# A planned order for a four-layer block on one core: idle products on TensorE in the first part, and another list of turns

## The chip, the core and the metric

The kernel runs on one NeuronCore of a Trainium2 chip. The metric is the device time of one execution in microseconds (us). The core has five engines that run their own instruction streams and meet at semaphores: TensorE (PE, whose weight loads are listed as PEld), VectorE (DVE), ScalarE (ACT), GpSimd (POOL) and SyncE (SP, which here only issues DMAs). [...]

## The reference

The input x has 16 sequences of 512 tokens by 256 features, all in f32. Each sequence passes four residual layers, each behind a layer norm, and no sequence needs another.

```python
x = x + attention(layernorm(x))     # 16 heads of 16, causal softmax, inner RMS norm
x = x + routed(layernorm(x))        # base product + shared low rank + 6 routed low ranks, best 2
x = x + scan(layernorm(x))          # conv of 4, silu, softplus; 16 states for each feature
x = x + routed(layernorm(x))        # the same weights as before

def scan_step(h, dt, bt, ct, xt):   # over 512 tokens
    h = exp(A * dt) * h + dt * xt * bt
    return h, sum_over_states(h * ct)
```

## The kernel before, in words

A sequence lies in SBUF as x with 4 tiles of 128 tokens. Its work is cut into some 376 steps (`plan.op`), each on one engine, each a small group of instructions with an estimated cost, the buffers that it reads and writes, and a place in PSUM or SBUF that it must hold. The functions `attention`, `routed` and `scan` only record the steps of one sequence; `order()` then plays all 16 sequences through at the estimated costs and puts out one order of all 6016 steps. A step is taken when its inputs are done, its engine is free and its buffers have places; among those that could go, the one with the smallest turn goes first. The turn is the sequence's entry of `STARTS` plus the step's entry of `TURNS`, which is one list of 376 numbers for all sequences. `OVER` and `CHANGE` are two more numbers of this rule (how far a kept engine may be overrun, and what a change of ScalarE's table counts). In the end the steps are issued in that order. The order is fixed at build time: on the chip each engine goes through its own list and waits where a semaphore is not yet there.

Up to four sequences are under way at a time, since x has four places. The places that matter here:

- PSUM has four banks called "one", for nearly everything (projections, transposes, sums, and the decays of the scan), and one group of four banks called "sc", for the attention scores of four heads.
- bc, the broadcast B and C of the scan, has one place. dd, what the scan works on, has five.

The steps around the change, with their lines:

- Attention makes the scores twice. First `four` (L566 the products of four heads into sc, L568 the mask added) is followed by a row maximum on VectorE (L637, into negm). The maxima are turned (L645) and added to the queries (qm, L650), the scores are made again (L566, L568), ScalarE takes the exponentials (L585, into pt), and L590 weighs the values with them. L601 turns the result back, L608 divides.
- `products` (L474) is the helper for all other products, so L474 stands for many of them: wq, wk, wv, wo, the base product and so on.
- `normalised` (L481 to L494): statistics on VectorE, a power on POOL, xh on ScalarE; L505 transposes xh, L508 copies it out of PSUM.
- The scan: SP writes dt and dt times x to DRAM (L816, L819), the small few too (L829), reads it back broadcast as bc (L830), and reads 32 slices dd of 512 KB broadcast over the states (L849). POOL multiplies (L856), ScalarE makes the decays into a bank "one" (L861), VectorE scans (L864), POOL multiplies again (L867), TensorE sums over states (L874), VectorE applies the gate (L880).
- Four groups of setup instructions (`setups`) are not steps of the plan. They are issued when the first step that needs them comes up. The second, `for_attention`, holds the loads and the scaling of the weights, and two products (L359, and wo with sg).

Of the kernel before, what the change touches and what calls it, by code (L numbers as in the profile page):

```python
# [10 lines left out]
F32 = mybir.dt.float32  # L11
# [6 lines left out]
P = 128  # L18
NEG = -1.0e30


OVER, CHANGE = 2.3, 97.0
STARTS = (
    0, 149, 234, 338, 413, 521, 619, 700, 790, 888, 996, 1074, 1174, 1263, 1369, 1447,
)
TURNS = (
    322, 924, 785, 870, 705, 84, 602, 525, 716, 736, 780, 829, 935, 688, 816, 888, 551, 888, 569, 780, 1037,
    1058, 780, 1053, 1052, 703, 823, 720, 796, 729, 794, 743, 758, 752, 822, 761, 826, 825, 945, 858, 844,
    656, 460, 479, 710, 820, 765, 711, 797, 755, 722, 823, 826, 738, 806, 840, 1808, 856, 863, 744, 849,
    851, 744, 788, 833, 754, 788, 766, 751, 859, 885, 1705, 883, 866, 807, 1037, 1066, 872, 1095, 1116, 757,  # L30
    814, 758, 845, 775, 829, 775, 854, 787, 878, 778, 819, 785, 833, 801, 850, 564, 392, 477, 669, 771, 810,
    720, 849, 837, 723, 824, 834, 729, 799, 814, 1625, 859, 798, 753, 898, 878, 758, 869, 924, 763, 873,
    814, 774, 828, 887, 1728, 845, 870, 913, 1017, 867, 1025, 795, 747, 619, 606, 834, 836, 824, 854, 204,
    875, 859, 701, 653, 760, 785, 601, 885, 649, 900, 844, 1052, 761, 625, 294, 465, 645, 644, 492, 604,
    701, 765, 811, 782, 660, 0, 531, 800, 645, 687, 566, 570, 613, 641, 518, 510, 470, 703, 660, 743, 1034,
    946, 605, 616, 676, 882, 619, 1044, 680, 1060, 712, 805, 957, 1000, 1101, 663, 941, 1101, 623, 890,
    1153, 849, 783, 616, 695, 622, 701, 684, 886, 650, 959, 803, 1136, 745, 727, 871, 1195, 973, 1019, 873,
    1211, 928, 818, 818, 937, 1046, 783, 1096, 904, 1208, 761, 767, 840, 962, 673, 1117, 931, 1159, 919,
    869, 880, 1059, 1081, 860, 1141, 944, 1257, 903, 867, 907, 1191, 989, 1264, 959, 1209, 1026, 890, 917,
    932, 1162, 952, 1293, 1071, 1366, 917, 930, 1018, 1268, 989, 1331, 1144, 1482, 1193, 1207, 930, 961,  # L40
    1168, 1480, 1042, 1195, 1009, 1344, 962, 968, 1052, 1231, 1060, 1264, 1093, 1321, 1019, 995, 969, 1128,
    1304, 1126, 1316, 1047, 1366, 973, 998, 1084, 1144, 1062, 1295, 1240, 1372, 1060, 993, 1019, 1122, 1311,
    1039, 1297, 1013, 1390, 1064, 1037, 1188, 1297, 1133, 1352, 996, 1349, 1058, 988, 1069, 1158, 1353,
    1153, 1350, 1021, 1424, 1076, 1045, 1055, 1230, 997, 1317, 1028, 1427, 999, 1130, 1032, 1059, 1037,
    1031, 1050, 1016, 1108, 1187, 528, 1091, 1082, 1153, 1067, 1132, 1266, 1209, 1446, 1077, 1275, 1141,
    1558, 1308, 1166, 904, 1004, 1071, 1242, 1188, 1479, 1564, 1511,
)


class Buf:  # L50


    def __init__(self, plan, res, make):
        self.plan, self.res, self.make = plan, res, make
        self.tile, self.users, self.taken = None, 0, False
        self.done = {}
# [11 lines left out]
class Plan:  # L68
# [5 lines left out]

    def __init__(self, places):
        self.places, self.ops, self.seq, self.stage = dict(places), [], 0, 0
# [46 lines left out]
    def order(self):  # L126

        first = {}
        for o in self.ops:
            o.turn = STARTS[o.seq] + (TURNS or [0] * len(self.ops))[o.num - first.setdefault(o.seq, o.num)]  # L130
        free, busy, table, link, port = dict(self.places), {}, None, 0.0, False
        kept = {}
        ready = {}
        for o in self.ops:
            ready.setdefault(o.eng, [])
            busy.setdefault(o.eng, False)
            if not o.left:
                bisect.insort(ready[o.eng], (o.turn, o.num, o))
        events, out = [], []
        now, tick = 0.0, 0  # L140
        while True:
            for eng, heap in ready.items():
                if busy[eng] or not heap:
                    continue
                until, what = kept.get(eng, (None, None))

                picked, turns = None, heap
                if eng == "ACT":
                    turns = sorted(heap, key=lambda i: (i[0] + CHANGE * (i[2].table not in (None, table)), i[1]))
                for item in turns:  # L150
                    if until is not None and not self.wanted(item[2], what):
                        cost = item[2].cost + 1.3 * (item[2].table not in (None, table))
                        if now + cost > until + OVER:
                            continue
                    need = {}
                    for b in item[2].bufs:
                        if not b.taken:
                            need[b.res] = need.get(b.res, 0) + 1
                    if not (item[2].port and port) and all(free[k] >= v for k, v in need.items()):
                        picked = item[2]  # L160
                        heap.remove(item)
                        break
                if picked is None:
                    continue
                o = picked
                for b in o.bufs:
                    if not b.taken:
                        b.taken = True
                        free[b.res] -= 1
                cost = o.cost  # L170
                if o.table is not None:
                    cost += 1.3 * (o.table != table)
                    table = o.table
                if until is not None and self.wanted(o, what):
                    del kept[eng]
                if isinstance(o.then, Op):
                    kept[o.then.eng] = (now + cost + o.lat, o.then)
                elif o.then is not None:
                    kept[o.then[0]] = (now + cost + o.lat, o.then[1])
                busy[eng] = True  # L180
                port = port or o.port
                out.append(o)
                end = now + cost
                done = end + o.lat
                if o.load:
                    link = max(link, end) + o.load
                    done = link + o.lat
                tick += 2
                heapq.heappush(events, (end, tick, "free", o))
                heapq.heappush(events, (done, tick + 1, "done", o))  # L190

            late = [eng for eng, (at, what) in kept.items() if at + 0.3 < now and not busy[eng]]
            for eng in late:
                del kept[eng]
            if late:
                continue
            if not events:
                if not kept:
                    break
                kept.clear()  # L200
                continue
            now = events[0][0]
            while events and events[0][0] <= now:
                _, _, kind, o = heapq.heappop(events)
                if kind == "free":
                    busy[o.eng] = False
                    if o.port:
                        port = False
                    continue
                for b in o.bufs:  # L210
                    b.users -= 1
                    if not b.users:
                        free[b.res] += 1
                for x in o.after:
                    x.left -= 1
                    if not x.left:
                        bisect.insort(ready[x.eng], (x.turn, x.num, x))
        assert len(out) == len(self.ops), "operations wait for each other's places"
        self.span = now
        return out  # L220


@with_exitstack
def tile_block(ctx: ExitStack, tc: tile.TileContext, a: dict, out: bass.AP):
# [4 lines left out]
    nc = tc.nc  # L229
# [16 lines left out]
    ps = ctx.enter_context(tc.tile_pool(name="ps", bufs=1, space=PSUM))  # L246
# [5 lines left out]
    def tile_of(name, shape, dtype=F32):  # L252
        return const.tile(shape, dtype, name=name)
# [7 lines left out]
    ident, identb = tile_of("ident", [P, P]), tile_of("identb", [P, P], BF)  # L261
# [166 lines left out]
    banks = {"one": (4, [P, 512]), "sc": (1, [P, G, 512])}  # L428
# [3 lines left out]
    plan = Plan(places)  # L432
# [463 lines left out]
    with tc.manual_schedule():  # L896
        done = 0
        for o in plan.order():

            while done < o.stage:  # L900
                setups[done]()
                done += 1
            o.fn()


# [44 lines left out]
```

## Time and profile before

| | before |
|---|---|
| time, median of 3 runs | 2061.71 us (2060.84 to 2065.83) |
| the profiled execution, its own time | 2066.51 us |
| its span, first to last instruction | 2064.7 us |
| busy PE / DVE / POOL / ACT | 1801.9 / 1513.4 / 1371.1 / 1194.0 us |
| mean granted TensorE clock | 0.954 |
| DMA | 316.35 MB, 153 GB/s mean |

Busy times are sums over the span, for one profiled execution. The page's slices cut the span into 40 equal parts and give each engine's busy share in tenths, with the granted TensorE clock (PEclk) below. A timeline row gives start, duration, engine, line, operation, operands and count; brackets hold the idle time just before it and what ended it. In the trace an f32 product that is no transpose appears as two records.

### The profile page before, as it was taken

How to read it: one execution, taken by the hardware profiler on the slowest of the kernel's cores; microseconds unless marked ns; L12 is line 12 of the kernel's file. 1: busy time of each engine (PE TensorE's matmuls, PEld its weight loads, DVE VectorE, ACT ScalarE, POOL GpSimd, SP SyncE). 2: the span in 40 equal slices, each digit the busy share in tenths (PEclk: the TensorE clock that was granted, in tenths of full speed). 3: DMA queues.
4: the chain of work that ended last, by engine and by line, in shares of the span. 5: the costliest groups of instructions: out<-in, count | busy, mean ns of one | idle time of the engine just before them, and what ended most of it. 6: DMA issues, size and time to landing. Idle time of an engine off the chain costs nothing. (4 is left out here: it accounts for less than half of the span.)

```text
span 2064.7 us, 34733 instructions
## 1 busy us (share of the span) xinstructions
PE 1801.9 (87%) x13253; PEld 953.8 (46%) x13253; DVE 1513.4 (73%) x2479; ACT 1194.0 (58%) x1685; POOL 1371.1 (66%) x814
## 2 busy tenths in 40 slices
PE   4788789999999999999999999999999999996455
PEld 2244344555455454545455454545554454544123
DVE  4335677878788787878788787878788787876563
ACT  2236556565666757565666667575666766564431
POOL 3001784949587685859597785859596785848693
PEclk8789899999999999999999999999999999998766
DMA  3000956848494866847494867849493957747791
GB/s 93 1 1 22 216 122 155 197 127 210 109 233 109 216 164 167 205 137 191 110 231 100 225 153 175 204 120 212 110 231 95 228 143 186 183 125 183 186 222 31
DMA packets 113064, 316.35 MB, mean 153 GB/s; under 512 B 17809, under 2 KB 36610, under 8 KB 112898
## 3 DMA queue, kind: packets, MB, share of 16 engines
q1 hardware_dynamic: 112194, 313.99, 62.5%
q8 instruction: 105, 1.72, 0.4%
q14 instruction: 61, 0.50, 0.1%
q10 hardware_dynamic: 704, 0.14, 0.0%
HBM read 287.87 MB, written 26.21 MB: 152 GB/s over the span
## 5 line engine op out<-in xcount | busy, mean ns | idle before, releaser
L864 DVE TENSOR_TENSOR_SCAN dd<-one,dd 128x512 f32<-128x512 f32 x512 | 607.9, 1212 | 185.2 <-ACT one L861 88.3
L856 POOL TENSOR_TENSOR dd<-dd,bc 128x1024 f32<-128x1024 f32 x256 | 603.6, 2361 | 194.0 <-DMA dd<-drows 156.8
L867 POOL TENSOR_TENSOR dd<-dd,bc 128x1024 f32<-128x1024 f32 x256 | 601.9, 2358 | 86.2 <-DVE dd L864 80.4
L637 DVE TENSOR_REDUCE negm<-sc 128x4 f32<-128x512 f32 (+3 forms) x256 | 380.4, 1486 | 154.0 <-PE sc L568 153.7
L861 ACT ACTIVATE one<-dd,am 128x512 f32<-128x512 f32 x512 | 344.3, 689 | 249.4 <-DVE dd L864 108.9
L585 ACT ACTIVATE pt<-sc 128x2048 f32<-128x2048 f32 (+3 forms) x256 | 316.3, 1235 | 189.0 <-PE sc L568 187.8
L487 POOL TENSOR_SCALAR rs<-mv 128x4 f32<-128x4 f32 x64 | 12.3, 193 | 364.2 <-DVE mv L482 361.4
L566 PE MATMUL sc<-qm,kT 32*128 32x512 f32 (+3 forms) x2048 | 214.1, 488 | 37.8 <-ACT pt L585 28.4
L566 PE MATMUL sc<-kT,qT 32*128 32x128 f32 (+3 forms) x2048 | 217.0, 494 | 30.5 <-DVE negm L637 25.9
L568 PEld LDWEIGHTS <-identb 128*128 128x128 bf16 x2048 | 117.4, 98 | 232.4 <-issue 217.2
L874 PE MATMUL one<-dd,ysel 128*32 128x512 f32 x1024 | 172.7, 633 | 55.5 <-POOL dd L867 46.4
L590 PE MATMUL one<-pt,vv 128*32 128x512 f32 (+3 forms) x2048 | 191.6, 449 | 8.1 <-DVE dd L864 7.9
L566 PEld LDWEIGHTS sc<-qm,kT 32*128 32x128 f32 x2048 | 80.9, 185 | 181.5 <-ACT pt L585 120.4
L474 PE MATMUL one<-base,xtR 128*128 128x256 f32 x512 | 139.5, 395 | 18.6 <-DVE dd L864 18.0
L566 PEld LDWEIGHTS sc<-kT,qT 32*128 32x128 f32 x2048 | 82.0, 187 | 156.8 <-DVE negm L637 63.3
L494 ACT ACTIVATE xhR<-x,nm,rs 128x256 f32<-128x256 f32 x192 | 99.4, 588 | 53.2 <-POOL nm L490 53.1
L528 DVE TENSOR_TENSOR x<-one,x 128x512 f32<-128x512 f32 x128 | 86.4, 675 | 34.7 <-PE one L474 34.5
L474 PEld LDWEIGHTS one<-base,xtR 128*128 128x128 f32 x512 | 94.5, 194 | 36.8 <-DVE dd L864 21.5
L481 DVE BATCH_NORM_STATS2 st<-x 128x6 f32<-128x256 f32 x256 | 103.7, 405 | 4.8 <-DMA x<-in_x_dram 4.1
L568 PE MATMUL sc<-mask_q,identb 128*128 128x128 bf16 x1024 | 103.7, 225 | 0.0
L568 PE MATMUL sc<-mask_k,identb 128*128 128x128 bf16 x1024 | 102.8, 224 | 0.0
L505 PE MATMUL one<-ident,xhR 128*128 128x128 f32 x384 | 61.9, 290 | 35.2 <-ACT xhR L494 27.7
(132 smaller groups left out, 2449.4 us busy)
## 6 DMA issues: line engine op xcount, KB each, us to landing
dd<-drows SPq DMA_DIRECT2D x512, 512.0 KB
x<-in_x_dram SPq DMA_DIRECT2D x16, 512.0 KB
drows<-dt SPq DMA_DIRECT2D x32, 256.0 KB
drows<-sg SPq DMA_DIRECT2D x32, 256.0 KB
bc<-brows SPq DMA_DIRECT2D x16, 512.0 KB
out_dram<-x SPq DMA_DIRECT2D x16, 512.0 KB
brows<-few SPq DMA_DIRECT2D x16, 64.0 KB
wo<-in_Wo_dram SPq DMA_DIRECT2D x2, 256.0 KB
```

Source lines behind the costliest of these rows:

```text
L474: nc.tensor.matmul(o[:, lo:hi], lhsT=lhsT, rhs=rhs, start=n == 0, stop=n == len(todo) - 1)
L481: nc.vector.bn_stats(st()[:, t, :], x()[:, t, :])
L566: nc.tensor.matmul(sc()[:, g, 0:n], lhsT=lhsT(g), rhs=rhs(g), start=True, stop=False)
L568: nc.tensor.matmul(sc()[:, g, at : at + P], lhsT=identb, rhs=mask, start=False, stop=True)
L585: o.then = op("ACT", act(G * n), lambda pt=pt, sc=sc, n=n: nc.scalar.activation(pt(), sc()[:, :, 0:n], AF.Exp), r=[sc], w=[pt], table="exp")
L590: nc.tensor.matmul(av()[rows(g), kt * P : T], lhsT=vals()[:, kt, G * j + g, :], rhs=pt()[:, g, :], start=kt == 0, stop=kt == NT - 1,)
L637: o.then = op("DVE", dve(G * n), lambda t=t, n=n, sc=sc, nm=nm, s=s: nc.vector.tensor_reduce(nm()[:, t, :, 1 - s, 0:1], sc()[:, :, 0:n], A ...
L856: op("POOL", pool(1024), lambda dd=dd: nc.gpsimd.tensor_tensor(dd()[:, :, 1, :], dd()[:, :, 1, :], both(0), ALU.mult), port=True, r=[(bc, ...
L861: op("ACT", act(512) + 0.07, lambda i=i, k=k, dd=dd, dec=dec: nc.scalar.activation(dec(), dd()[:, i, 0, :], AF.Exp, scale=am[:, k + 4 * i ...
L864: op("DVE", 1.22, lambda i=i, dd=dd, dec=dec: nc.vector.tensor_tensor_scan(dd()[:, i, 1, :], dec(), dd()[:, i, 1, :], 0.0, ALU.mult, ALU.a ...
L867: op("POOL", pool(1024), lambda dd=dd: nc.gpsimd.tensor_tensor(dd()[:, :, 1, :], dd()[:, :, 1, :], both(1), ALU.mult), port=True, r=[(bc, ...
L874: nc.tensor.matmul(sums()[rows(g), :], lhsT=ysel[:, m, :], rhs=four[g]()[:, g % 2, 1, :], start=m == 0, stop=m == 3)
```

## The change

The list of turns and the starts are replaced, with `OVER` and `CHANGE`. The other part is new: `order()` now also keeps the stretches in which TensorE is busy in the played schedule and how many banks "one" are free over time. `resting` goes through the schedule's first part (to `START`, in the schedule's own time) and looks at each rest of TensorE: where a rest is long enough for an idle product, a bank "one" is free, and TensorE was busy for less than a set share of the time just before, it counts one idle product for the step that follows. When the steps are issued, each such product multiplies the identity with itself, 256 columns in f32, into a bank "one" that nothing reads. This makes 63 idle products. None is issued ahead of the first setup.

```diff
-OVER, CHANGE = 2.3, 97.0
-STARTS = ( 0, 149, 234, 338, 413, 521, 619, ...
-TURNS = ( 322, 924, 785, 870, 705, 84, ...
+OVER, CHANGE = 2.2, 380.0
+STARTS = ( 0, 388, 628, 931, 1235, 1513, ...
+TURNS = ( 964, 2212, 2292, 2200, 2062, 1448, ...
...
+    SPAN, BUSY, IDLE, EDGE, START = 3.4, 0.72, 0.45, 0.1, 330.0
...
+        runs, room = [], [(0.0, free["one"])]
...
+                if eng == "PE":
+                    runs.append((now, end, o))
...
+        self.rests = self.resting(runs, room)
         return out
+
+    def resting(self, runs, room):
+        rests, last, at, k = {}, [], 0.0, 0
+        for begin, end, o in runs:
+            if begin > self.START:
+                break
+            while at + self.IDLE + self.EDGE <= begin:
+                while k + 1 < len(room) and room[k + 1][0] <= at:
+                    k += 1
+                i, free = k + 1, room[k][1]
+                while i < len(room) and room[i][0] < at + self.IDLE + self.EDGE:
+                    free = min(free, room[i][1])
+                    i += 1
+                last = [x for x in last if x[1] > at - self.SPAN]
+                worked = sum(b - max(a, at - self.SPAN) for a, b in last)
+                if free > 0 and worked < self.BUSY * self.SPAN:
+                    rests[o.num] = rests.get(o.num, 0) + 1
+                    last.append((at, at + self.IDLE))
+                    at += self.IDLE
+                else:
+                    at += self.EDGE
+            last.append((begin, end))
+            at = max(at, end)
+        return rests
...
                 setups[done]()
                 done += 1
+            for _ in range(plan.rests.get(o.num, 0) if done else 0):
+                one = ps.tile([P, 512], F32, tag="one", name="one", bufs=banks["one"][0])
+                nc.tensor.matmul(one[:, 0 : 2 * P], lhsT=ident, rhs=ident.unsqueeze(1).to_broadcast([P, 2, P]), start=True, stop=True)
             o.fn()
```

The new order is close to the old one. Sequences begin and end at nearly the same shares of TensorE's steps; of 1520 steps on TensorE 85% stand in the same order as before, on VectorE 68%, on ScalarE 74%, on POOL and SP 81 and 82%. In the changed kernel all lines from the class Plan on are some 5 to 43 lower down in the file; the texts use the numbers of the kernel before unless they say otherwise.

## The prediction

> **What bounds the kernel now.** I read the page's slices first, to split the run into stages; then the busy time and clock of each stretch of 50 us; then TensorE's own waits in the middle; then the timelines of the two ends. The page's slices:
>
> ```profile
> PE   4788789999999999999999999999999999996455
> PEclk8789899999999999999999999999999999998766
> ```
>
> There are three stages: a first part of some 330 us in which TensorE is neither full nor at full clock, a middle to about 1850 us at nine tenths and more, and a tail. Stretches of 50 us (busy PE, PEld, DVE, ACT, POOL, then clock, DMA share, GB/s):
>
> ```profile
> 50.00:100.00 50.00, 36.74 (x272) 15.17 (x276) 13.93 (x13) 14.32 (x15) 0.00 (x0) 0.74 0.00 1
> 100.00:150.00 50.00, 41.27 (x310) 20.72 (x303) 13.89 (x28) 17.25 (x21) 0.00 (x0) 0.82 0.00 1
> ...
> 1100.00:1150.00 50.00, 47.65 (x348) 25.56 (x347) 38.76 (x67) 33.64 (x50) 24.99 (x21) 1.00 0.41 108
> ...
> 1950.00:2000.00 50.00, 22.41 (x91) 11.20 (x89) 31.06 (x51) 16.89 (x28) 45.25 (x23) 0.71 0.95 221
> ```
>
> From 50 to 150 us TensorE is busiest by far and runs at 0.74 and 0.82 of its clock, while GpSimd and DMA do nothing. In the middle TensorE bounds at full clock. In the tail it is GpSimd (45 of 50 us). TensorE's timeline shows how the clock is lost:
>
> ```profile
> 96.17 1.24 PE L566 MATMUL sc<-kT,qT 32*128 32x256 f32 x8 [2.38 <-DVE negm L637]
> 97.34 0.60 PE L568 MATMUL sc<-mask_q,identb 128*128 128x128 bf16 x4
> 99.26 1.66 PE L566 MATMUL sc<-kT,qT 32*128 32x384 f32 x8 [1.32 <-DVE negm L637]
> ...
> 114.27 3.73 PE L474 MATMUL one<-xtA,wq 128*128 128x512 f32 x4
> 117.93 0.93 PE L566 MATMUL sc<-qm,kT 32*128 32x384 f32 x8
> ```
>
> The tile sc exists once, so product and row maximum alternate, and TensorE rests in every maximum. The granted clock is 0.50 from 94 to 118 us: the product of 384 columns takes 1.66 us at 99.26 and 0.93 at 117.93. All of this lies on the path. In the middle, TensorE's own waits from 350 to 1850 us (total, times, longest) are:
>
> ```profile
> PE sc L566 <- ACT pt L585: 20.8, 66, 2.0
> PE one L474 <- DVE dd L864: 18.0, 13, 1.4
> PE one L645 <- DVE dd L864: 9.2, 13, 0.9
> PE one L590 <- DVE dd L864: 7.0, 12, 0.6
> ```
>
> The last three wait for a PSUM bank "one" that a scan on VectorE still holds, once in each sequence. The loads of x that wait for a place run from 400.4 to 1670.6 us in 11 steps, so a sequence takes 115.5 us.
>
> **The change part by part.** 1. *Idle products.* The changed program has 63 of them, 256 columns in f32. Four such real products (wv, 33.03 us) take 1.95 us, so one costs 0.49 us warm; at half clock the two of wo,sg took 2.08 us with their latency, so about 0.97.
>
> What they can win is the cold work repriced at its own warm rows. 44.6 to 66.4 us: products, masks, turns and the wq projection sum to 15.99 us cold and 9.06 warm, 6.9 less. 96.2 to 117.9: the same mix, 6.9 less. 214 to 225: 3.3. 251 to 254: 1.6. 285 to 292: 2.8. In the first two nothing else is busy, so I count 13.8 in full. The other three (7.7) lie beside the first scans, where the DMA share is about 1.0 and POOL fills up; I count half, 3.9, and keep 0 and 7.7 as ends.
>
> [...] With one to three idle products in each maximum (the order has 3 behind a score product of 512 columns, 1 behind one of 128 or 256, 2 or 3 behind 384), these stretches rise from below 0.6 to about 0.75 busy. They fit: the gaps at warm rates are 0.8, 1.3, 1.9 and 2.4 us against 0.49 to 1.47.
>
> What they cost. *The start.* 19 of them stand behind wo,sg and ahead of the first transposes of xhA. The schedule's own times know nothing of the setup, and on the chip those transposes do not wait for data: xhA is ready at 10.8 us.
>
> ```profile
> 20.80 1.80 PE L505 MATMUL one<-ident,xhA 128*128 128x128 f32 x8
> ...
> 25.32 3.37 PE L474 MATMUL one<-xtA,wq 128*128 128x512 f32 x4
> 28.49 3.95 PE L474 MATMUL one<-xtA,wk 128*128 128x512 f32 x8
> 32.37 0.50 PE L566 MATMUL sc<-kT,qT 32*128 32x128 f32 x8
> ```
>
> From 21.0 us: the clock came back after 6 us of gapless work (111.85 to 117.9), so four are cold (3.9 us) and 15 warm (7.4): transposes at 32.3. Then four transposes 0.6, copy 0.59, three xhA activations that ScalarE now has between the two copies 1.55, copy 0.59, and wk, wq, four transposes, wk at warm rates 6.5: first score product at 42.2 instead of 32.4, 9.8 later less small overlaps, so +9.5. Behind the last idle product stand all of attention's products; VectorE and ScalarE wait for those. *The other 44.* Those in maxima are covered by VectorE's reduce; without that cover each is 0.49. 11 of them wait for a bank that ScalarE or VectorE must release, the last around the first scans. No row shows such a wait; the nearest is a real product's wait for L864, 0.5 to 2.2 us in the first part. I take +2 in all (0 to 8).
>
> Sum of the first part: -13.8 -3.9 +9.5 +2 = -6.2. The middle is bound by TensorE, so the shift reaches the end.
>
> 2. *The order in the middle.* Each engine keeps its instructions[...]. Three moves bear on the shown waits. The value product behind a score product is moved one score product later (L590), which puts 0.64 us of filler (pt of 256 columns) just ahead of the L474 base product that waits 1.4 for its bank. On VectorE the gate product L880, which frees the bank "sums", goes ahead of the two qm steps, so the 0.7 us waits at L645 may shrink. Against it, scans are now grouped two and two ahead of row maxima, so a maximum may come 1.2 us (one L864) later, with sc and all of TensorE behind it. SP's loads of dd follow the new order of POOL, at equal numbers. Ends: -2 us (all three bank waits gone, and some of pt) to +2 (a new wait of 1.2 to 2.4); I take -0.5 for 13 sequences, -6.5, near the filler's size.
>
> 3. *The tail.* The load of bc for the last sequence waits for its only buffer:
>
> ```profile
> 1937.82 4.63 POOL L867 TENSOR_TENSOR dd<-dd,bc 128x1024 f32<-128x1024 f32 x2 [2.94 <-DVE dd L864]
> 1947.17 2.35 POOL L856 TENSOR_TENSOR dd<-dd,bc 128x1024 f32<-128x1024 f32 x1 [4.72 <-DMA bc<-brows]
> 1952.97 2.34 POOL L856 TENSOR_TENSOR dd<-dd,bc 128x1024 f32<-128x1024 f32 x1 [3.45 <-DMA dd<-drows]
> ```
>
> SP issues it at 1942.47, when L867 ends. Two dd loads stand ahead of it now; in the changed order they stand behind it, with the second drows write (L819), and land two transfers later (0.5 MB at the 230 GB/s of the slices is 2.3 us each). POOL then starts at about 1951.8 and is fed 3 us later for good. POOL's order before that point is also changed and may end sequence 14 earlier; waits of 4.33, 1.83 and 2.94 us stand there. I take +1.5 (-6 to +5).
>
> Sum: -6.2 -6.5 +1.5 = -11.2. The profiled execution spans 2064.7 us and took 2066.5, 0.2% above the median of 2061.7; against the median this gives 2050.
>
> **The rivals.** *A better middle.* If the order takes 1.5 us off each sequence's 6 us of waits, 13 times: -19.5 -6.2 +1.5, 2038, and 2034 with the late cold stretches in full. For it: bank waits are what the moves touch. Against it: the moves are of one place mostly.
>
> *Slower: a new wait in the middle.* A pair of scans (2.4 us) ahead of a row maximum that TensorE waits for, in each of 13 sequences. At 1.5 us each it is +19.5 -6.2 +1.5: 2076. It decides from 1.0 us a sequence on, where it outweighs the first part beyond 0.3%. For it: a maximum's release of sc is already a wait of TensorE's weight loads. Against it: in the middle, TensorE itself waited for negm once.
>
> *Only the cost.* The clock stays low in spite of the idle products, or TensorE's saving runs into the scans: +9.5 +4, 2075. [...] *It cancels.* The changed program has the products, but the start's 9.5 eats the gain and the order is neutral: 2060.
>
> **How the numbers follow.** A measurement of this kernel tells 0.3%, 6.2 us, from no change. Forecast (2040 to 2058) 0.42, of it 0.05 within 0.3%; better middle 0.16; cancels 0.11; new wait 0.22; only the cost 0.09. Faster 0.53, same 0.16, slower 0.31. The range 2027 to 2077 leaves out a tenth on either side; the forecast's own range is 2040 to 2058.
>
> **What would show it.** Right: clock 1.00 from 35 to 330 us; the first score product at about 42 us, and the wq projection that ended at 118 us some 4 us earlier; a sequence at 115.0 us; the last scan's first POOL step waiting for dd, not bc. Wrong: transposes at 21 us (the 19 are hidden), clock 0.5 in the maxima, a period of 116 us or more, or new waits of idle products for banks near 300 us.

## The result, and the profile after

| | before | after |
|---|---|---|
| time, median of 4 runs each | 2061.97 us (2060.84 to 2065.83) | 2028.09 us (2024.89 to 2031.13) |
| ratio, 95% interval | 1 | 0.9832 (0.9812 to 0.9852) |
| span of the profiled execution | 2064.7 us | 2023.1 us |
| mean granted TensorE clock | 0.954 | 0.973 |

The change makes the kernel 33.9 us faster by the medians. The direction was forecast, the size (11.2 us) was not. The two profiled executions differ by 41.6 us, because the one before is 4.5 us slower than its median and the one after 3.2 us faster. So a shift read from the traces is up to some 8 us too large at the end. It can also be off at a single point: five later runs with the old order in the first 200 us (m2 to m6 below) have the last exponential of sequence 0 at 129.2 to 131.8 us, the profile before has it at 134.1. Ratios are used for sizes, traces for places.

Lines of the changed kernel are 40 higher from attention on (L864 is L904, L566 is L606 and so on); the idle products are L945. The page's slices of the changed kernel, TensorE's busy share and its clock:

```profile
PE   5889889999999999999999999999999999996544
PEclk9999999999999999999999999999999999998866
```

The clock is at nine tenths or more in the first 36 slices; before, four of the first five stood at 7 or 8. Stretches of 50 us of the changed kernel (PE, PEld, DVE, ACT, POOL, clock, DMA share, GB/s):

```profile
50.00:100.00 50.00, 40.37 (x345) 19.93 (x344) 18.69 (x17) 14.34 (x15) 0.00 (x0) 1.00 0.00 1
100.00:150.00 50.00, 42.95 (x352) 23.95 (x352) 17.94 (x34) 18.87 (x25) 2.65 (x5) 1.00 0.00 1
```

From 50 to 150 us the clock went from 0.74 and 0.82 to 1.00, and TensorE is busy 5 us longer, with idle products among its work. POOL already has its first work before 150 us. TensorE's timeline in the maxima, at the place shown before:

```profile
96.01 0.71 PE L606 MATMUL sc<-kT,qT 32*128 32x256 f32 x8 [1.03 <-DVE negm L677]
...
96.89 0.65 PE L945 MATMUL one<-ident 128*128 128x256 f32 x2
...
109.50 1.94 PE L514 MATMUL one<-xtA,wq 128*128 128x512 f32 x4
```

One idle product (two records) stands in the maximum, the wait behind it is short, and the products have their warm durations: 0.71 us where there were 1.24, and wq 1.94 where it took 3.73. The start of TensorE's timeline shows the price:

```profile
20.82 10.24 PE L945 MATMUL one<-ident 128*128 128x256 f32 x38
30.89 1.04 PE L545 MATMUL one<-ident,xhA 128*128 128x128 f32 x8
...
39.94 0.50 PE L606 MATMUL sc<-kT,qT 32*128 32x128 f32 x8
```

The 19 products ahead of the first transposes last 10.24 us, and the first score product begins at 39.94 us instead of 32.37. TensorE's own waits from 400 to 1800 us, first before, then after (us in total, times, longest):

```profile
PE one L474 <- DVE dd L864: 16.7, 12, 1.4
PE one L645 <- DVE dd L864: 8.3, 12, 0.9
PE one L505 <- DVE dd L864: 6.6, 13, 0.5
PE one L874 <- issue: 6.0, 12, 0.5
...
PE one L874 <- POOL dd L867: 2.2, 12, 0.2
```

```profile
PE one L514 <- DVE dd L904: 13.1, 24, 1.1
PE one L914 <- POOL dd L907: 12.0, 24, 1.1
PE one L545 <- DVE dd L904: 10.4, 24, 0.6
...
PE one L685 <- DVE dd L904: 6.8, 12, 0.9
```

The bank waits have not gone: the three for VectorE's scans come to 31.6 us before and 30.3 after. The longest of L474 fell from 1.4 to 1.1 us, that of L645 stayed at 0.9, the waits of xhR's transposes (L505, now L545) grew, and the waits of the sums over states (L874, now L914) went from 8.2 us (6.0 of them "issue", which the profile puts down to nothing) to 12.0 for POOL. Yet the loads of x that wait for a place now run from 394.5 to 1648.8 us in 11 steps, 114.0 us for a sequence instead of 115.5. Six more traces below with this order in the middle (e2, e3, e4, f1, f2, s2) give 114.1 to 114.3 us, four with the old one (e1, m3, m5, s1) 115.4 to 115.7; so the gain is nearer to 1.3 us a sequence. From the first exponential of sequence 3 to that of sequence 15, twelve sequences, before and after (us, busy PE, PEld, DVE, ACT, POOL, clock, DMA share, GB/s):

```profile
398.71:1784.73 1386.02, 1305.38 (x9937) 697.27 (x9938) 1123.42 (x1825) 889.29 (x1260) 1025.46 (x601) 1.00 0.70 170
```

```profile
382.30:1751.57 1369.27, 1296.05 (x9936) 696.24 (x9936) 1117.41 (x1825) 887.81 (x1261) 1025.21 (x601) 1.00 0.71 172
```

In these two traces TensorE is idle for 0.6 us less in each sequence, and busy for 0.8 us less with the same work. Most of the busy part is in the sums over states: L874 alone is busy for 118.4 us of this stretch before and 110.2 after.

Where the shift arises, by each sequence's first exponential (L585), the first and last POOL step of a scan, and the end; the runs e1 and e2 below split the change into its two parts:

| us | before | after | idle products alone | order alone |
|---|---|---|---|---|
| last pt of sequence 0 | 134.1 | -6.0 | -6.6 | -3.5 |
| scan of sequence 0, first step | 214.7 | -6.3 | -6.0 | -4.1 |
| scan of sequence 0, last step | 311.4 | -21.1 | -9.6 | -16.7 |
| first pt of sequence 3 | 398.7 | -16.4 | -10.1 | -12.4 |
| first pt of sequence 15 | 1784.7 | -33.2 | -8.2 | -27.1 |
| scan of sequence 14, last step | 1940.1 | -43.3 | -7.5 | -37.1 |
| scan of sequence 15, first step | 1947.2 | -35.2 | -7.5 | -28.4 |
| end | 2064.7 | -41.6 | -8.9 | -35.6 |

### The profile page after: what moved, and what is told of

Read it like the earlier page. It is cut to its first block, busy times and chain, and to the rows that moved or that the text cites. A ratio compares the mean times of both kernels' runs of the same rounds, so it can differ in the third digit from the quotient of the medians.

```text
span 2023.1 us, 34985 instructions
## 1 busy us (share of the span) xinstructions
PE 1794.7 (89%) x13379; PEld 962.0 (48%) x13379; DVE 1504.3 (74%) x2479; ACT 1189.4 (59%) x1683; POOL 1371.1 (68%) x814
## 5 line engine op out<-in xcount | busy, mean ns | idle before, releaser
L904 DVE TENSOR_TENSOR_SCAN dd<-one,dd 128x512 f32<-128x512 f32 x512 | 607.1, 1211 | 182.2 <-ACT one L901 84.3
L677 DVE TENSOR_REDUCE negm<-sc 128x4 f32<-128x1024 f32 (+3 forms) x256 | 380.0, 1484 | 166.1 <-PE sc L608 166.0
L606 PE MATMUL sc<-qm,kT 32*128 32x512 f32 (+3 forms) x2048 | 210.3, 480 | 27.1 <-ACT pt L625 20.7
L606 PE MATMUL sc<-kT,qT 32*128 32x128 f32 (+3 forms) x2048 | 210.3, 480 | 20.9 <-DVE negm L677 16.7
L914 PE MATMUL one<-dd,ysel 128*32 128x512 f32 x1024 | 167.3, 632 | 63.2 <-POOL dd L907 48.6
L608 PEld LDWEIGHTS <-identb 128*128 128x128 bf16 x2048 | 115.6, 97 | 224.8 <-issue 209.4
L630 PE MATMUL one<-pt,vv 128*32 128x512 f32 (+3 forms) x2048 | 186.5, 443 | 7.7 <-DVE dd L904 7.6
L606 PEld LDWEIGHTS sc<-qm,kT 32*128 32x128 f32 x2048 | 80.0, 182 | 161.2 <-ACT pt L625 114.8
L606 PEld LDWEIGHTS sc<-kT,qT 32*128 32x128 f32 x2048 | 80.0, 182 | 148.6 <-DVE negm L677 50.3
L514 PEld LDWEIGHTS one<-base,xtR 128*128 128x128 f32 x512 | 92.9, 191 | 34.2 <-DVE dd L904 20.9
L545 PE MATMUL one<-ident,xhR 128*128 128x128 f32 x384 | 61.6, 291 | 38.6 <-ACT xhR L534 26.5
```

The lines of the kernel that those rows point to most:

```text
L514: nc.tensor.matmul(o[:, lo:hi], lhsT=lhsT, rhs=rhs, start=n == 0, stop=n == len(todo) - 1)
L606: nc.tensor.matmul(sc()[:, g, 0:n], lhsT=lhsT(g), rhs=rhs(g), start=True, stop=False)
L608: nc.tensor.matmul(sc()[:, g, at : at + P], lhsT=identb, rhs=mask, start=False, stop=True)
L630: nc.tensor.matmul(av()[rows(g), kt * P : T], lhsT=vals()[:, kt, G * j + g, :], rhs=pt()[:, g, :], start=kt == 0, stop=kt == NT - 1,)
L677: o.then = op("DVE", dve(G * n), lambda t=t, n=n, sc=sc, nm=nm, s=s: nc.vector.tensor_reduce(nm()[:, t, :, 1 - s, 0:1], sc()[:, :, 0:n], A ...
L904: op("DVE", 1.22, lambda i=i, dd=dd, dec=dec: nc.vector.tensor_tensor_scan(dd()[:, i, 1, :], dec(), dd()[:, i, 1, :], 0.0, ALU.mult, ALU.a ...
```

## The experiments

**The two parts apart.** Edits: e1 keeps the changed program and gives it the old lists; e2 keeps the new lists and drops the idle products.

```diff
 e1_idle_only
-OVER, CHANGE = 2.2, 380.0      (STARTS and TURNS likewise)
+OVER, CHANGE = 2.3, 97.0
 e2_order_only
-        return rests
+        return {}
```

Expected of e1: 

> The order of the kernel before, with the idle products added by the same rule (again 63, nearly at the same places). Theory A (the forecast's own split: clock saving less the cost of the 19 at the start, and the rest of the gain is the order): about 6 us faster than before, 2056; TensorE's clock 1.00 in the first part, the first exponential of sequence 3 (362.5 us before, 346.8 after) at about 356, the middle at 115.5 us a sequence, and the tail as long as before. Theory B (the idle products are worth all of the 16 us gained in the first part, the late cold stretches in full): about 17 us faster, 2045, that exponential at about 347.

Expected of e2: 

> The changed order without any idle product. Theory A: 28 us faster than before, 2034; the clock falls to 0.5 in the first part as before, yet the filling of the pipeline from 240 to 350 us is about 10 us shorter than before, the middle takes 114.0 us a sequence, the tail is 8 us shorter. Theory B: 17 us faster, 2045: middle and tail as in the changed kernel, nothing gained before 350 us.

(The 362.5 and 346.8 us in the first of these are the last exponential of sequence 2. The first one of sequence 3 is at 398.7 us before, at 382.3 after and at 388.6 in e1.)

Measured: e1 0.9969 (0.9959 to 0.9979), 6 us faster; e2 0.9859 (0.9843 to 0.9876), 29 us faster. Their product, 0.9828, agrees with the whole change's 0.9832. The idle products give what the first part's sum said; the list of turns gives four fifths of the gain. In e1 the clock still falls in the first scans (0.90 from 250 to 300 us). In e2 it falls in the maxima, as before (0.81 and 0.87 from 50 to 150 us, before 0.74 and 0.82), but from 250 to 400 us it is 1.00 without any idle product. Stretches of e1, then of e2:

```profile
250.00:300.00 50.00, 44.28 (x330) 24.69 (x328) 36.53 (x64) 28.59 (x42) 40.52 (x25) 0.90 0.50 118
```

```profile
250.00:300.00 50.00, 44.65 (x356) 25.71 (x352) 41.32 (x67) 30.72 (x45) 45.98 (x27) 1.00 0.64 148
```

**The 19 at the start, and idle products everywhere.** e3 drops the 19 ahead of the first transposes, e4 lets idle products stand over the whole schedule (223 of them).

```diff
 e3_no_head
+        rests.pop(runs[0][2].num, None)
         return rests
 e4_all
-    SPAN, BUSY, IDLE, EDGE, START = 3.4, 0.72, 0.45, 0.1, 330.0
+    SPAN, BUSY, IDLE, EDGE, START = 3.4, 0.72, 0.45, 0.1, 5000.0
```

Expected of e3: 

> The changed kernel without the 19 idle products ahead of the first transposes, 44 remain. If these 19 lie on the path as forecast (9.5 us, less the cold products that come back, about 2): 7 to 8 us faster than the changed kernel, about 2020. If what waits for them is absorbed later, by the first scans' transfers: as the changed kernel, 2028.

Expected of e4: 

> The changed kernel with the rule for idle products over the whole schedule: 223 in place of 63, all the new ones in the tail, where TensorE runs at 0.5 to 0.85 of its clock. The last chain (sums over states, two products with their transposes) holds some 12 us of cold work, so full clock there is worth up to 6 us: 2022. If the 8 to 20 idle products that stand ahead of single steps come late against the schedule's times, each costs 0.49 us on the path: 2030 to 2045.

Measured: e3 0.9799 (0.9784 to 0.9814), 7 us faster than the changed kernel by the ratios (with some 5 us of uncertainty) and 9 by the medians, so the start's cost was real and on the path. e4 0.9983 (0.9975 to 0.9990), some 31 us slower than the changed kernel and beyond both cases of its expectation. Its first 1800 us are as in the changed kernel; the loss is in the tail, as its timeline and TensorE's waits from 1800 to 2060 us show:

```profile
1934.24 10.82 PE L945 MATMUL one<-ident 128*128 128x256 f32 x36 [7.39 <-DVE z L777]
```

```profile
PE one L945 <- DVE dd L904: 31.9, 11, 9.0
```

An idle product needs a bank, and in the tail the scans hold the banks later than the played schedule says. So TensorE's queue stands behind a product that nobody needs, 31.9 us for banks of the scans and 7.4 for one that VectorE still reads, and the scan's sums (L914) stand behind them. In the changed kernel the 63 idle products wait for a bank once, 0.7 us, and one of ScalarE's decays waits 2.3 us for a bank that an idle product holds: the "+2" of the forecast.

**Where the order pays.** Each kernel here issues a written list of the 6016 steps, made of the old and the new order: s1 has the new one up to the first exponential of sequence 3 and the old one from there, s2 the new one up to that of sequence 15.

```diff
+ORDER = ( ...
-        for o in plan.order():
+        plan.order()
+        for o in (plan.ops[n] for n in ORDER):
```

Expected of s1: 

> The changed kernel (idle products too) up to the first exponential of sequence 3; from there on all remaining steps in the order of the kernel before. If the three stages add up (16 us gained in the filling, 13 to 15 in the middle, 8 in the tail): 16 us faster than before, 2046, with 115.5 us a sequence in the middle and the old tail. If the old order gives the filling's lead back (its waits are set by the scans' transfers): 2055 or more.

Expected of s2: 

> The changed kernel up to the first exponential of sequence 15; all steps after it in the order of the kernel before. If the tail's 8 us come from its own order: 2034 to 2036, the last scan's first POOL step back at a bc that waits for the scan before it. If they come from the middle's lead alone: 2028.

Measured: s1 0.9928 (0.9916 to 0.9941), s2 0.9867 (0.9854 to 0.9881). With 0.9832 for all, the ratios split the gain into 14.8 us up to sequence 3, 12.6 in the middle and 7.2 in the tail, with some 3, 4 and 5 us of uncertainty. In s1 the shift stays at -17.2 to -20.3 us from sequence 3 to the end and a sequence takes 115.5 us, as before: the middle's gain is the middle's own order. In s2 the last scan's first step waits 4.6 us for bc again.

**One move of the middle at a time.** m1 is the changed kernel with the gate product of the first half (L880) put back behind the two qm steps in every sequence. m2 is the kernel before with the value products (L590) of one value tile one score product later, m6 the kernel before with only the gate product moved forward. All are edits of such a list.

```diff
 m1_gate_back (on the changed kernel)
-    ... gate (L880), qm, qm ...
+    ... qm, qm, gate (L880) ...
 m2_av_later (on the kernel before)
-    ... value products (L590), score product ...
+    ... score product, value products (L590) ...
 m6_gate_forward (on the kernel before)
-    ... qm, qm, gate (L880) ...
+    ... gate (L880), qm, qm ...
```

Expected of m1: 

> The changed kernel with one VectorE step of each sequence put back: the gate product L880 of the first half again behind the two qm steps, where it stood before. If its earlier release of the bank sums is what the middle gains: TensorE's waits at L645 and L505 for a scan grow by 0.3 to 0.6 us in a sequence, 2032 to 2036. If not: 2028, 114.0 us a sequence.

Expected of m2: 

> The kernel before (no idle products) with one part of the new order alone: the value products L590 of the first value tile of each sequence each one score product later, as in the changed order. If this filler is what shortens the base product's wait for its bank: that wait falls from 1.4 to about 0.8 us, 2054. If the wait only moves elsewhere: 2062.

Expected of m6: 

> The kernel before with one VectorE step of each sequence moved: the gate product L880 of the first half ahead of the two qm steps, as in the changed order. If the earlier release of the bank is worth the same here as the 0.9 us a sequence that putting it back cost: 2050. If it is worth that only together with the other moves: 2057 to 2062.

Measured: m1 0.9862 (0.9848 to 0.9875), 6.2 us slower than the changed kernel (with some 5 us of uncertainty), with 114.9 us for a sequence where the seven traces of the new middle have 114.0 to 114.3. m2 0.9976 (0.9966 to 0.9986), 4.9 us faster than before, with 115.1 us for a sequence instead of 115.5. m6 1.0025 (1.0013 to 1.0036), 5 us slower than before, with 115.6 us for a sequence; that is beyond both cases of its expectation, and where the 5 us arise was not found. So the gate's place is worth 0.5 us (by the ratios) to 0.7 us (by the traces) of a sequence within the new order, and in the old one it gains nothing. TensorE's waits from 400 to 1800 us, of m1 and then of m2:

```profile
PE one L799 <- DVE dd L1158: 16.3, 24, 1.0
...
PE one L939 <- DVE dd L1158: 7.4, 12, 0.9
```

```profile
PE one L728 <- DVE dd L1118: 9.9, 13, 1.0
```

In m1 (L799 is L505, L939 is L645, L1158 is L864) the late gate shows in the waits of xhR's transposes, 16.3 us instead of 10.4 or 0.5 us more in each sequence, and not in the turns of the maxima, 7.4 instead of 6.8, where the forecast had looked for it. In m2 (L728 is L474, L1118 is L864) the base product's waits fall from 16.7 to 9.9 us, as the forecast had it.

**The scan's own order.** m3 is the kernel before with the scan's own steps of sequences 0, 1 and 13 to 15 in the new order among themselves.

Expected of m3: 

> The kernel before (no idle products) with one part of the new order: in sequences 0, 1, 13, 14 and 15 the scan's own steps, from the load of bc on, keep their places in the list but follow each other as in the changed order. If the scan's own order is what shortens the filling (12 us without idle products) and the tail (8 us): up to 15 us faster than before, 2047, POOL's last scan step of sequence 0 near 300 in place of 311 us. If these gains come from the order of attention and projections around the scans: 2060 to 2064.

Measured: 1.0105 (1.0089 to 1.0121), 22 us slower than before, beyond both cases of its expectation. Up to sequence 3 it gains 1.8 us, no more than the profiles scatter; in the tail it loses, and the last scan begins 15 us later than before. The scan's order by itself is not the source.

**One end at a time.** m4 and m5 are the kernel before with the new order only from sequence 0's first scan step to the first exponential of sequence 3 (m4), or only from the first exponential of sequence 15 on (m5).

Expected of m4: 

> The kernel before (no idle products) with the new order in one stretch alone: from the first POOL step of sequence 0's scan (215 us) to the first exponential of sequence 3 (399 us) all steps follow the changed order, ahead of it and behind it the old one. If the 8 us that the order alone gains there come from that stretch's order as a whole: 2054, clock 1.00 from 224 us on. If they rest on the small lead that the order brings into it from before 215 us: 2060 to 2062.

Expected of m5: 

> The kernel before with the changed order from the first exponential of sequence 15 on, nothing else changed. If the tail's gain is its own order's, as taking it away showed: 8 us faster, 2054, sequence 14's last scan step some 7 to 11 us earlier. If it needs the changed middle ahead of it: 2060.

Measured: m4 0.9973 (0.9966 to 0.9980), 5.6 us faster; m5 0.9968 (0.9961 to 0.9975), 6.6 us faster. The filling and the tail each pay alone, each a little less than the 8 us of its first case. Of the filling, the scan of sequence 0 tells most, from POOL's first step (L856) to the end of its last (L867); first the kernel before, then m4, then the changed kernel (PE, PEld, DVE, ACT, POOL, clock, DMA share, GB/s):

```profile
214.71:313.77 99.06, 83.64 (x652) 41.77 (x648) 68.18 (x93) 56.92 (x80) 82.46 (x42) 0.90 0.68 157
```

```profile
212.06:301.28 89.22, 76.05 (x581) 38.58 (x580) 65.53 (x90) 52.30 (x72) 78.27 (x37) 0.94 0.75 173
```

```profile
208.44:292.72 84.28, 73.84 (x590) 38.90 (x586) 64.84 (x89) 52.15 (x72) 78.36 (x37) 1.00 0.78 184
```

The scan takes 99.1, 89.2 and 84.3 us, and POOL is idle in it for 16.6, 10.9 and 5.9 us. The rest of the difference is other work of POOL, five instructions of 4 us, that no longer falls between its steps. What POOL waited for within this scan, before and after:

```profile
POOL dd L856 <- DMA dd<-drows: 8.8, 6, 3.3
POOL dd L867 <- DVE dd L864: 6.3, 5, 2.3
```

```profile
POOL dd L896 <- DMA dd<-drows: 4.4, 3, 2.1
POOL dd L907 <- DVE dd L904: 1.1, 3, 0.4
```

The tail, from the first exponential of sequence 15 to the end, in its five pieces (us):

| | before | after | m5 |
|---|---|---|---|
| to POOL's first step in the scan of sequence 14 | 59.0 | 57.9 | 56.5 |
| that scan, to the end of its last step | 98.7 | 89.7 | 90.4 |
| from there to the first step of the last scan | 4.7 | 12.8 | 13.0 |
| the last scan | 81.5 | 77.7 | 77.2 |
| from there to the end | 36.1 | 33.5 | 33.7 |

The scan of sequence 14 is 9 us shorter. Its waits in POOL, before and after:

```profile
POOL dd L856 <- DMA dd<-drows: 9.6, 5, 4.3
POOL dd L867 <- DVE dd L864: 6.3, 3, 2.9
```

```profile
POOL dd L896 <- DMA dd<-drows: 4.9, 2, 2.5
POOL dd L907 <- DVE dd L904: 4.0, 1, 4.0
```

The next scan then begins 12.8 us after it instead of 4.7, with a wait for dd and not for bc, and so gives 8 of the 9 us back. POOL's timeline there, in the changed kernel:

```profile
1896.81 2.35 POOL L907 TENSOR_TENSOR dd<-dd,bc 128x1024 f32<-128x1024 f32 x1 [3.97 <-DVE dd L904]
...
1911.95 2.35 POOL L896 TENSOR_TENSOR dd<-dd,bc 128x1024 f32<-128x1024 f32 x1 [3.15 <-DMA dd<-drows]
```

What is left at the end comes mostly from the other pieces, in the changed kernel 1 us ahead of these, 4 in the last scan and 3 behind it. A part of the 4 is a normalisation of x (L487 to L490, 1.6 us on POOL) that now stands ahead of the last scan and not in it; the rest was not traced to a move.

**Can the start's cost be had for nothing?** In the setup TensorE waits until 18 us with nothing to do. f1 is e3 with 30 idle products right behind the first setup, where only the identity is needed. f2 is f1 with 6 more ahead of each of two late steps of the last sequence, the transposes of its last xhR and the last turn of hsc, where no scan holds a bank any more.

```diff
 f1_head_moved (on e3)
                 done += 1
+                for _ in range(30 if done == 1 else 0):
+                    one = ps.tile([P, 512], F32, tag="one", name="one", bufs=banks["one"][0])
+                    nc.tensor.matmul(one[:, 0 : 2 * P], lhsT=ident, rhs=..., start=True, stop=True)
 f2_and_end (on f1)
+        rests[5998] = rests[6009] = 6
         return rests
```

Expected of f1: 

> The changed kernel without the 19 idle products ahead of the first transposes; 30 idle products stand instead right behind the setup that makes the identity, where TensorE waits 18 us for the weights and nothing is behind them. If they end before that wait does, they cost nothing and the setup's products, the first transposes and projections run at full clock: 2 to 3 us faster than without the 19, 2016. If the clock falls again before 18 us or was not lost there: 2019.

Expected of f2: 

> As the kernel with the moved 30, and 6 idle products each ahead of the last transposes of xhR and of the last turn of hsc, in waits of 5.6 and 5.1 us, where nothing but the last chain is left and all banks are free. 6 take 2.9 us at full clock and 5.8 at half. If the clock holds: 3 to 4 us of cold products saved, 2013. If they run cold: as the other, or 1 us slower.

Measured: f1 0.9785 (0.9770 to 0.9799), f2 0.9770 (0.9756 to 0.9784), 2015.61 us. The start of TensorE's timeline in f1 (L946 are idle products), and one row of f2:

```profile
1.34 16.03 PE L946 MATMUL one<-ident 128*128 128x256 f32 x60 [1.34 <-POOL ident masks.py:199]
...
18.96 1.10 PE L515 MATMUL one<-wo,sg 128*128 128x256 f32 x4 [0.69 <-DMA cw<-in_conv_w_dram]
...
28.95 0.50 PE L607 MATMUL sc<-kT,qT 32*128 32x128 f32 x8
```

```profile
19.01 2.04 PE L516 MATMUL one<-wo,sg 128*128 128x256 f32 x4 [0.69 <-DMA cw<-in_conv_w_dram]
```

In both, the 30 idle products end before TensorE is wanted (in f1 at 17.37 us, where its next product starts at 18.08) and cost nothing. In f1 they also help: wo,sg takes 1.10 us instead of 2.08, and the first score product comes at 28.95 us, 11.0 earlier than in the changed kernel and 1.7 earlier than in e3. In f2, with the same 30, the granted clock of the first 50 us is 0.97, wo,sg takes 2.04 us, and the first score product comes at 30.37 us, close to e3's 30.64. Against e3 f1 gains some 3 us by the ratios (1 by the medians), and f2 some 3 more (2.3 by the medians); their intervals overlap, so only the distance of f2 to the changed kernel, 12 to 13 us, is sure. At the other end, from the transposes of the last xhR on, f2 takes 20.9 us, the changed kernel 22.2, e2 22.3 and f1 23.5.

## Why the prediction was right or wrong

The forecast of 2040 to 2058 us failed at the order of the steps and not at the idle products. In the middle the order was counted at -6.5 us and gave 12.6; in the filling it had no term and m4, with the order of that stretch alone, gained 5.6; in the tail it was counted at +1.5 and gave some 7 us of gain.

**The idle products: the sum right, in part by luck.** The forecast gave -13.8 us for the first two cold stretches and -3.9 for the later ones, against +9.5 at the start and +2 for the rest: -6.2. e1, with the idle products alone, is 6.4 us faster (4.3 to 8.5). The start came in at 7.6 us (39.94 against 32.37) instead of 9.8, and e3 confirms it as 7 to 9. At the last exponential of sequence 0 the six traces with the 63 products stand at 127.2 to 128.3 us, some 3 us ahead of the five with the old order named above; the 6.0 of the table is against a profile that was late there. So the first cold stretches gave some 10 to 11 us, not 13.8: a smaller cost met a smaller saving. That the clock would hold at some 0.75 busy, which the -13.8 and the -3.9 need, was the author's estimate. The runs bear it out for the maxima: between 50 and 150 us the clock is 1.00 in e1 against 0.74 and 0.82 before, in one and the same order, and in the changed kernel the two stretches that were cold are 0.76 and 0.77 busy at 1.00. Before, no rest of TensorE in them was over 2.4 us, and the clock stood at 0.50.

**The filling: wrong by omission.** The sum had -3.9 for the late cold stretches and no term for the order between 215 and 400 us. There the order alone brings e2 to -12.4 us at sequence 3, and m4, with that piece only, is 5.6 us faster at the end. POOL's idle time within the scan of sequence 0, which the forecast did not price, fell from 16.6 us to 8.1 in e2 and 10.9 in m4. The new order also removes the cold stretches at 251 and 285 us by itself, in e2 with no idle product at all (clock 1.00 from 250 to 310 us, before 0.91, 0.88 and 0.95 in stretches of 20 us); those were counted as the idle products' work, at half. The first part gave 14.8 us by s1's ratio where the sum said 6.2. Which single move in the filling carries it stays open: m3 rules out the scan's own order as sufficient, and no smaller piece than m4's was tried.

**The order in the middle: the term that was mis-sized.** "I take -0.5 for 13 sequences, -6.5": it was -1.3 a sequence by the traces, 13 to 19 us from sequence 3 to sequence 15, and 12.6 us by the ratios. A part of it was named for the right reason: m2 shows the later value products to be worth 0.4 us of a sequence, and they act on the base product's wait as said. As large a part was the gate product, 0.5 to 0.7 us of a sequence (m1), which acts on xhR's transposes and not on L645 as said. And each was priced as if the other moves did not matter, while m6 shows no gain from the gate's move in the old order. The two are seen in runs that start from different kernels, so they need not add. Nor do waits tell it all: of 1.4 us a sequence between the two profiles 0.8 are busy time, most of it in the sums over states, and with the gate back (m1) this part stays. What made it busy for less was not separated. The fear against it, a row maximum behind a pair of scans, did not come: TensorE waits for negm once in the middle, 0.3 us.

**The tail: the wait foreseen, a named gain left at nothing.** "+1.5 (-6 to +5)": the last scan's first step does wait for dd instead of bc, and later than said (12.8 us behind the scan before it, where the forecast's 1951.8 is 9.4). But "may end sequence 14 earlier" was counted at nothing, and it was 9 us, more than the wait took. The waits of 4.33, 1.83 and 2.94 us that the text named there, 9.1 in all, became one of 3.97. And "fed 3 us later for good" did not hold: the last scan and what follows it are 6.4 us shorter. m5 alone is 6.6 us faster and s2, without it, 7.2 slower.

**The rivals.** *A better middle* was the nearest, with its -1.5 us a sequence where 1.3 were measured: the time came out 6 to 10 us below its 2034 to 2038, since it too had no term for the filling's order and +1.5 for the tail. *A new wait in the middle* did not come. *Only the cost* fails at the clock of 1.00, and *it cancels* fails at e2: the order was not neutral. Of the signs named for being right, the clock of 1.00, the first score product near 42 us (39.94) and the last scan's wait for dd came; the period of 115.0 us did not (114.0).

## What to carry to other kernels

Where an order is rewritten, price the filling and the draining of the pipeline with the same care as its steady middle: here they held 5.6 and 6.6 us. The idle time of GpSimd within one scan, 16.6 us of 99 in the filling and 18.9 of 99 in the tail, was the room there; a wait that is named but counted at nothing is a term that is missing. Compare such waits over the same work, not over the same microseconds: with a kernel that has come 34 us ahead, a fixed stretch of time holds other steps. A move that frees a buffer earlier is not worth a fixed price: the same gate product was worth 6 us in one order and nothing in another. In these runs the idle products that held TensorE's clock cost little or nothing where TensorE waited for another engine and a bank was free (the setup, the row maxima). Ahead of ready work they cost most of their own time (7 to 9 us of 10.2), and where banks were held they cost more than that (e4, some 31 us).

## What the runs showed of the hardware

TensorE's busy time and its granted clock around the two cold stretches, in steps of 10 us:

| us | before: busy us | before: clock | after: busy us | after: clock |
|---|---|---|---|---|
| 40 to 50 | 4.73 | 0.64 | 8.59 | 1.00 |
| 50 to 60 | 5.80 | 0.50 | 7.34 | 1.00 |
| 60 to 70 | 9.11 | 0.66 | 8.61 | 1.00 |
| 70 to 80 | 7.88 | 0.85 | 8.51 | 1.00 |
| 80 to 90 | 9.06 | 0.98 | 8.51 | 1.00 |
| 90 to 100 | 4.89 | 0.70 | 7.40 | 1.00 |
| 100 to 110 | 6.08 | 0.50 | 7.88 | 1.00 |
| 110 to 120 | 8.62 | 0.60 | 8.63 | 1.00 |
| 120 to 130 | 7.13 | 1.00 | 8.10 | 1.00 |

Over the cold stretches as a whole the kernel before is 15.14 us busy from 44.6 to 66.4 us and 15.21 from 94 to 118, a share of 0.69 and 0.63, at 0.50; the changed kernel is 16.54 and 18.47 us busy there, a share of 0.76 and 0.77, at 1.00. So in this case the forecast's 0.75 busy in the maxima went with the full clock. The busy share of a stretch does not tell its clock by itself: the kernel before has 1.00 at 7.13 us from 120 to 130 us and 0.60 at 8.62 us from 110 to 120. What decides about the clock these rows do not show.

At the start the durations tell more than the recorded clock. In the kernel before it stands at 1.00 from 18 to 21 us, and wo,sg takes 2.08 us there, where it takes 1.10 in f1. The forecast's half clock for wo,sg is an estimate from that duration.
